# Layer 0 attention as two streams side by side: eight target tiles on ScalarE and GpSimd, seventeen on VectorE

## The chip, the cores and the metric

The kernel runs on one core of a Trainium2 chip. The metric is the device time of one execution in microseconds. TensorE is called PE here (its weight loads PEld), VectorE DVE, ScalarE ACT, GpSimd POOL, and SyncE SP, as in the profile.

## The reference

A graph of 3,125 nodes with 256 features and 103,125 edges passes through four layers. Each layer has a graph attention, a mixing block and an expert network, with layer norms between them. The change is in layer 0, where the graph attention is:

```
proj  = (xn @ Wp.T).reshape(-1, 8, 32)                 # 8 heads
s     = leaky_relu(scores_src[src] + scores_trg[trg], 0.2)
exp_s = exp(s - max(s));  attn = exp_s / (segment_sum(exp_s, trg)[trg] + 1e-16)
out   = segment_sum(proj[src] * attn, trg)
out   = elu(out + xn @ Wskip.T + bias)
x     = x + out + mix(xn)
x     = x + routed_experts(layernorm(layernorm(x)))    # top 2 of 8 experts
```

## The kernel before

The graph is made dense. The function `counts` builds a matrix of how many edges go from each source node to each target node, and stores it in DRAM as bytes, `count_d`, with 25 tiles of 128 source nodes (the last has 53) against all 3,125 targets. Targets are counted in 25 tiles of 125. For some blocks of 250 targets, named by `FAR`, it also stores the counts as bf16 in `far_d`. The order in which blocks are counted is `BLOCKS`.

The attention (`dense_pairs`) then computes, for each pair of heads, the sum over source tiles of (weight matrix) x (projected features `zs`). The weight of an edge is exp of a leaky ReLU of two scores. It can be made in two ways. *Near* (`weigh`, line 1904) uses that exp(leaky_relu(a + b)) is, up to factors that are put elsewhere, the maximum of a row `q` and a column `bar`; one VectorE instruction takes that maximum and multiplies by the counts. *Far* uses logarithms: ScalarE does a Relu (line 1986) and an Exp (line 1987), and GpSimd multiplies by the counts (line 1988).

Before the change there are three chunks of target tiles, `CHUNKS0`: two of 8 and one of 9. In each chunk the first six tiles (750 columns) are near, and the last two or three (250 or 375 columns) far. For each chunk the kernel loops over four pairs of heads; one chunk and one pair of heads is called a unit here, and there are 12. In each unit it loops over 25 source tiles: load the counts, weigh two heads near and two far, and multiply. The matmuls (line 1971) put one head into columns 0 to 63 of the array and the other into 64 to 127, and so go in pairs. The first step of a unit reads the row `q_head` in SBUF; ScalarE then copies it to PSUM (line 1993, `q_near`), and the other 24 steps read it there:

```
q = qs[i][:K] if near is None else near[:K, i, :]
pts.append(self.weigh(wp, q, bar[:K, t, h], a, NQ, K, width=NQ))
```

Only PE's order is written by hand (`manual_schedule`); a scheduler decides that of the other engines. The far products of a step are multiplied one step late. `finish` transposes the sums and divides them (lines 1940 to 1945); its pieces are spread over the next unit's steps. After the four units of a chunk, `then` is called: `gnn0_out` (the skip product, line 739, and an ELU, lines 746 to 852) and `gate0` (two layer norms in one, transposes at line 2600, the router's product with Wr, the two best experts by `first_max`, and their shares, lines 2612 to 2616). It is not written as pieces; the scheduler mixes it with the next chunk's units. After the last chunk comes the routed expert network, which needs every tile's shares; its weights are loaded over the SP and ACT queues when the attention's memory is free.

Of the kernel before, what the change touches and what calls it, by code (L numbers as in the profile page):

```python
# [10 lines left out]
F32 = mybir.dt.float32  # L11
# [38 lines left out]
CHUNKS0 = [(0, 2), (8, 2), (16, 3)]  # L50
FAR = [3, 7, 11, 12]
BLOCKS = [3, 0, 7, 1, 11, 2, 12, 4, 5, 6, 8, 9, 10]
# [1410 lines left out]
class Dense(Net):  # L1463
# [223 lines left out]
    def counts(self, pieces, later):  # L1687
# [4 lines left out]
        self.far_d = self.dram.tile([NS, P, 7 * TP], BF16, name="far_d")  # L1692
# [225 lines left out]
    def dense_pairs(self, att, nodes, then):  # L1918


        nc, tc = self.nc, self.tc
        H, D = 8, 32
        W = D + 1
        NQ = 6 * TP
        zs, bar, q_d, log_s, log_d = nodes
        with ExitStack() as s:
            wq = s.enter_context(tc.tile_pool(name="daq", bufs=4))
            wa = s.enter_context(tc.tile_pool(name="daa", bufs=4))
            wp = s.enter_context(tc.tile_pool(name="dap", bufs=6))
            wo = s.enter_context(tc.tile_pool(name="dao", bufs=3))  # L1930
            we = s.enter_context(tc.tile_pool(name="dae", bufs=2))
            ps_q = s.enter_context(tc.tile_pool(name="dapq", bufs=1, space=PSUM))
            ps_t = s.enter_context(tc.tile_pool(name="dapt", bufs=1, space=PSUM))
            ps = s.enter_context(tc.tile_pool(name="dapp", bufs=4, space=PSUM))

            def finish(os, parts, h0):
                for o, (t, nt) in zip(os, parts):
                    p = ps_t.tile([P, 3, P], F32, name="p_t")[:TP]
                    for k in range(nt):
                        nc.tensor.transpose(p[:, k, :], o[:, k * TP:(k + 1) * TP], self.ident)  # L1940
                    v = p[:, :nt].rearrange("p t (j d) -> p t j d", d=64)
                    inv = wo.tile([TP, 3, 2], F32, name="inv")[:, :nt]
                    nc.vector.tensor_scalar(inv, v[:, :, :, D], 1e-30, None, op0=OP.max)
                    nc.vector.reciprocal(inv, inv)
                    nc.vector.tensor_mul(att[:, t:t + nt, h0 * D:(h0 + 2) * D].rearrange("p t (j d) -> p t j d", d=D),
                                         v[:, :, :, :D], inv[:, :, :, None].to_broadcast([TP, nt, 2, D]))
                    yield

            work = iter(())
            for t0, last in CHUNKS0:  # L1950
                d0, n = t0 * TP, NQ + last * TP
                for h0 in range(0, H, 2):
                    qs, logs = [], []
                    m = n - NQ
                    for i in range(2):
                        qs.append(wq.tile([P, NQ], F32, name="q_head"))
                        nc.sync.dma_start(qs[i], dview(q_d, (h0 + i) * N + d0, [[0, P], [1, NQ]]))
                        logs.append(wq.tile([P, 3 * TP], F32, name="q_log"))
                        nc.sync.dma_start(logs[i][:, :m], dview(log_d, (h0 + i) * N + d0 + NQ, [[0, P], [1, m]]))
                    near = None  # L1960
                    accs = {}

                    def sums(t, K, pts, banks):
                        for b in banks:
                            if t == 0:
                                accs[b] = ps.tile([P, 4, P], F32, name="p_o").rearrange("p a b -> p (a b)")
                            cols = last * TP if b == 2 else 3 * TP
                            for i in range(2):
                                z = (h0 + i) * W
                                at = 0 if b == 2 else b * 3 * TP  # L1970
                                nc.tensor.matmul(accs[b][64 * i:64 * i + 64, :cols], zs[:K, t, z:z + 64], pts[i][:K, at:at + cols],  # L1971
                                                 start=(t == 0), stop=(t == NS - 1))

                    with tc.manual_schedule(engines={mybir.EngineType.PE}):
                        late = None
                        for t in range(NS):
                            a, K = self.count_tile(wa, t, d0, NQ, False, NQ)
                            a_far = wa.tile([P, 3 * TP], BF16, name="a_far")
                            nc.sync.dma_start(a_far[:K, :m], self.far_d[t, :K, t0 // 8 * 250:t0 // 8 * 250 + m])
                            pts, far = [], []  # L1980
                            for i in range(2):
                                h = slice(h0 + i, h0 + i + 1)
                                q = qs[i][:K] if near is None else near[:K, i, :]
                                pts.append(self.weigh(wp, q, bar[:K, t, h], a, NQ, K, width=NQ))
                                f = wp.tile([P, 3 * TP], F32, name="pt_far")
                                nc.scalar.activation(f[:K, :m], logs[i][:K, :m], AF.Relu, bias=log_s[:K, 0, t, h])  # L1986
                                nc.scalar.activation(f[:K, :m], f[:K, :m], AF.Exp, bias=log_s[:K, 1, t, h], scale=1.0 - 0.2)  # L1987
                                nc.gpsimd.tensor_tensor(f[:K, :m], f[:K, :m], a_far[:K, :m], OP.mult)  # L1988
                                far.append(f)
                            if near is None:  # L1990
                                near = ps_q.tile([P, 2, NQ], F32, name="q_near")
                                for i in range(2):
                                    nc.scalar.activation(near[:, i, :], qs[i], AF.Copy)
                            sums(t, K, pts, (0, 1))
                            if late:
                                sums(*late, (2,))
                            late = t, K, far
                            next(work, None)
                        sums(*late, (2,))
                    parts = [(t0, 3), (t0 + 3, 3), (t0 + 6, last)]  # L2000
                    os = []
                    for b, (_, nt) in enumerate(parts):
                        os.append(wo.tile([P, 3 * TP], F32, name="o", bufs=4))
                        nc.scalar.activation(os[b][:, :nt * TP], accs[b][:, :nt * TP], AF.Copy)
                    work = finish(os, parts, h0)
                for _ in work:
                    pass
                then(we, ps, t0, 6 + last)
# [576 lines left out]
    def gate0(self, ps, x, xn, xT, xn_d, gate, t0, nt):  # L2585

        nc = self.nc
        E = 8
        wr, br, g, b, ones, share = gate
        ts = slice(t0, t0 + nt)  # L2590
        with self.tc.tile_pool(name="gate", bufs=1) as w:
            v = w.tile([TP, nt, E], F32, name="score")
            for a, na in GROUPS:
                if t0 <= a < t0 + nt:
                    self.layernorm_twice(xn, x, (a, na))
                    self.part_dma(nc.sync, xn_d.rearrange("(p t) f -> p t f", p=TP)[:, a:a + na, :], xn[:, a:a + na, :])
                    for k in range(KC):
                        p = ps.tile([P, 4, P], F32, name="p_o").rearrange("p a b -> p (a b)")
                        for t in range(na):
                            nc.tensor.transpose(p[:, t * TP:(t + 1) * TP], xn[:, a + t, k * P:(k + 1) * P], self.ident[:TP, :TP])  # L2600
                        nc.vector.tensor_scalar(xT[:, k, a * TP:(a + na) * TP], p[:, :na * TP], g[:, k:k + 1], b[:, k:k + 1],
                                                op0=OP.mult, op1=OP.add)
                    p = ps.tile([P, 4, P], F32, name="p_o").rearrange("p a b -> p (a b)")[:TP, :na * E].rearrange("p (t e) -> p t e", e=E)
                    for t in range(na):
                        self.mm(p[:, t, :], [(xT[:, k, (a + t) * TP:(a + t + 1) * TP], wr[:, k, :]) for k in range(KC)])
                    nc.vector.tensor_add(v[:, a - t0:a - t0 + na, :], p, br[:, None, :].to_broadcast([TP, na, E]))
# [140 lines left out]
    def layers(self, x, xn, xT, out, late):  # L2747
        nc, tc = self.nc, self.tc
        xn_d = self.dram.tile([N, C], F32, name="xn_d")
        with tc.tile_pool(name="hold", bufs=1) as hold:  # L2750
            with tc.tile_pool(name="skip", bufs=1) as sp:
# [8 lines left out]
                def out0(w, ps, t0, nt):  # L2760
                    self.gnn0_out(w, ps, x, xT, xn, skip, t0, nt)
                    self.gate0(ps, x, xn, xT, xn_d, gate, t0, nt)
# [172 lines left out]
```

## Time and profile before

| What | Value |
|---|---|
| Time, median of 3 runs | 5298.61 us (5291.43 to 5307.18) |
| Profiled execution: its own time | 5292.8 us |
| Profiled execution: its span | 5291.0 us |
| Granted PE clock, mean over the span | 0.946 |
| PE, DVE, ACT, POOL busy over the span | 90%, 68%, 31%, 28% |
| Counting of layer 0 | about 125 to 390 us of the span |
| Attention of layer 0, first weigh to last share | 405.8 to 1137.7 us |

A line of the order in time reads: start in us, length in us, engine, line of the kernel, operation, out<-in, shape, and how many instructions were merged into it. Its bracket holds the idle time of the engine before it, and what ended that. In the costliest groups, the mean duration of one instruction contains its waiting inside the engine; how far two starts lie apart is read from the order in time.

### The profile page before, as it was taken

Reading aid. Unit: us, or ns where it says so; the run is one execution under the profiler, and the core shown is the slowest. Engines: PE = TensorE matmul, PEld = TensorE weight load, DVE = VectorE, ACT = ScalarE, POOL = GpSimd, SP = SyncE. Lnnn points to the kernel's source line nnn. Section 1 sums busy time; section 2 is a strip of 40 time slices with the busy share of each in tenths; the row PEclk is TensorE's granted clock in tenths of the full one; section 3 lists DMA queues with packets and bytes.
Section 4 is the critical chain, followed back from the end, with each engine's and each line's share of the span. In section 5 each row is a group of like instructions: output and inputs, shape, how many; then the busy total and the mean of one; then the engine's idle time right before and its main releaser. Section 6 shows DMA issues by size and latency. Waiting matters only on the chain. (4 is left out here: it accounts for less than half of the span.)

```text
span 5291.0 us, 71854 instructions
## 1 busy us (share of the span) xinstructions
PE 4781.0 (90%) x25640; PEld 2885.3 (55%) x25640; DVE 3583.2 (68%) x6095; ACT 1642.1 (31%) x3317; POOL 1507.7 (28%) x1804
## 2 busy tenths in 40 slices
PE   6798999979798899999999899999997888899878
PEld 4565554448654433368645333355665555555557
DVE  6888898865555699845434899932235887777753
ACT  2668787941242100110133000033332111333221
POOL 1206565734300000000001000000004777777733
PEclk8899999979899999999999999999998889999989
DMA  3764333342400111111000111010004656666645
GB/s 92 79 47 115 83 100 83 92 133 65 110 1 0 32 34 43 32 41 35 15 14 1 33 33 42 27 58 8 1 1 120 174 165 185 184 181 171 182 143 173
DMA packets 367496, 413.59 MB, mean 78 GB/s; under 512 B 168554, under 2 KB 300010, under 8 KB 366559
## 3 DMA queue, kind: packets, MB, share of 16 engines
q1 hardware_dynamic: 278794, 189.94, 15.7%
q0 software_dynamic: 53744, 171.34, 11.3%
q10 hardware_dynamic: 34593, 47.63, 2.9%
q8 instruction: 208, 3.41, 0.3%
q14 instruction: 157, 1.28, 0.1%
HBM read 356.74 MB, written 55.18 MB: 78 GB/s over the span
## 5 line engine op out<-in xcount | busy, mean ns | idle before, releaser
L1904 DVE SCALAR_TENSOR_TENSOR pt<-q_head,bar,a 128x750 f32<-128x750 f32 (+2 forms) x824 | 807.4, 1036 | 74.2 <-PE acc L2048 52.3
L2202 POOL DMA_INDIRECT z_edge<-tab,src_i x806 | 776.3, 963 | 266.8 <-issue 210.8
L2043 PE MATMUL acc<-pt,zs 128*64 128x375 f32 (+2 forms) x3200 | 602.6, 501 | 24.2 <-DVE pt L1904 23.9
L2270 PE MATMUL p_acc<-z_edge,oh 128*125 128x264 f32 x2044 | 539.4, 425 | 92.0 <-DVE z_edge L2261 91.7
L1988 POOL TENSOR_TENSOR pt_far<-pt_far,a_far 128x250 f32<-128x250 f32 (+1 forms) x600 | 450.4, 772 | 377.4 <-ACT pt_far L1987 367.5
L1971 PE MATMUL p_o<-pt,zs 128*64 128x375 f32 (+1 forms) x2400 | 527.0, 495 | 30.1 <-DVE pt L1904 29.2
L1904 DVE SCALAR_TENSOR_TENSOR pt<-q_near,bar,a 128x750 f32<-128x750 f32 (+1 forms) x576 | 533.1, 991 | 17.0 <-PE p_o L1971 10.7
L2270 PEld LDWEIGHTS p_acc<-z_edge,oh 128*125 128x125 f32 x2044 | 419.3, 209 | 192.0 <-DVE z_edge L2261 102.2
L2043 PEld LDWEIGHTS acc<-pt,zs 128*64 128x64 f32 (+1 forms) x3200 | 246.4, 136 | 357.1 <-issue 221.0
L1971 PEld LDWEIGHTS p_o<-pt,zs 128*64 128x64 f32 (+1 forms) x2400 | 216.4, 138 | 237.2 <-issue 132.9
L1277 DVE SCALAR_TENSOR_TENSOR x<-p_y,sm,x 125x256 f32<-125x256 f32 x200 | 96.7, 484 | 361.3 <-PE p_y L739 361.3
L1986 ACT ACTIVATE pt_far<-q_log,log_s 128x250 f32<-128x250 f32 (+1 forms) x600 | 290.0, 529 | 89.7 <-PE p_o L1971 74.3
L1971 PE MATMUL p_o<-pt_far,zs 128*64 128x250 f32 (+3 forms) x1200 | 313.2, 414 | 2.1 <-POOL pt_far L1988 2.0
L2048 PE MATMUL acc<-pt,zs 128*32 128x375 f32 (+2 forms) x3200 | 313.4, 497 | 0.0
L1987 ACT ACTIVATE pt_far<-pt_far,log_s 128x250 f32<-128x250 f32 (+1 forms) x600 | 287.6, 524 | 0.2
L2098 PE MATMUL acc<-zs,pt 128*125 128x257 f32 x1250 | 275.6, 383 | 11.7 <-issue 11.7
L2098 PEld LDWEIGHTS acc<-zs,pt 128*125 128x125 f32 x1250 | 234.7, 189 | 52.6 <-issue 14.5
L1261 ACT ACTIVATE h<-p_tr,bn 128x500 f32<-128x500 f32 (+1 forms) x224 | 161.8, 723 | 296.7 <-PE p_tr L739 296.7
L2261 DVE TENSOR_TENSOR z_edge<-z_edge,near_e 128x2112 f32<-128x2112 f32 (+1 forms) x101 | 236.5, 2341 | 18.6 <-ACT near_e L2253 18.6
L2057 ACT ACTIVATE o<-acc 128x375 f32<-128x375 f32 (+1 forms) x48 | 21.2, 493 | 608.3 <-DMA q_head<-q_g 330.3
L1063 POOL IOTA own<- 5x256 f32 x1 | 0.4, 356 | 720.7 <-PE acc L2048 720.7
L1904 DVE SCALAR_TENSOR_TENSOR pt<-q_all,bar,a 128x500 f32<-128x500 f32 (+3 forms) x175 | 119.1, 683 | 122.6 <-PE acc L2098 120.2
(547 smaller groups left out, 7856.6 us busy)
## 6 DMA issues: line engine op xcount, KB each, us to landing
a<-count_d SPq DMA_DIRECT2D x432, 93.8 KB
row<-dst_row SPq DMA_DIRECT2D x101, 224.0 KB
ef<-in_edge_s SPq DMA_DIRECT2D x101, 128.0 KB
z_edge<-tab,src_i POOLq DMA_INDIRECT x806
a_far<-far_d SPq DMA_DIRECT2D x192, 62.5 KB
count_d<-stage SPq DMA_DIRECT2D x12, 781.2 KB
q_head<-q_g SPq DMA_DIRECT2D x24, 375.0 KB
a_far<-far_d SPq DMA_DIRECT2D x96, 93.8 KB
```

The costliest lines, as they stand in the source:

```text
L1261: nc.scalar.activation(o[:, m, :n], p[:, :n], AF.Relu, bias=b[:, e, m:m + 1], scale=g[:, e, m:m + 1])
L1904: self.nc.vector.scalar_tensor_tensor(pt[:K, :n], q, bar, a[:K, :n], op0=OP.max, op1=OP.mult)
L1971: nc.tensor.matmul(accs[b][64 * i:64 * i + 64, :cols], zs[:K, t, z:z + 64], pts[i][:K, at:at + cols], start=(t == 0), stop=(t == NS - 1))
L1986: nc.scalar.activation(f[:K, :m], logs[i][:K, :m], AF.Relu, bias=log_s[:K, 0, t, h])
L1987: nc.scalar.activation(f[:K, :m], f[:K, :m], AF.Exp, bias=log_s[:K, 1, t, h], scale=1.0 - 0.2)
L1988: nc.gpsimd.tensor_tensor(f[:K, :m], f[:K, :m], a_far[:K, :m], OP.mult)
L2043: nc.tensor.matmul(acc[i // 2][64 * (i % 2):64 * (i % 2) + 64, b, :b1 - b0], zs[:K, t, i * W:i * W + 64], pts[i][:K, b0:b1], **st)
L2048: nc.tensor.matmul(acc[2][32 * i:32 * i + 32, b, :b1 - b0], zs[:K, t, z:z + 32], pts[i][:K, b0:b1], **st)
L2098: nc.tensor.matmul(acc[i], pt[:K, i * TP:(i + 1) * TP], zs[:K, t, :C + 1], start=(t == 0), stop=(t == NS - 1))
L2202: nc.gpsimd.indirect_dma_start(out=zs[i][:, j, :], out_offset=None, in_=table, in_offset=bass.IndirectOffsetOnAxis(ap=src[:, c0 + j:c0 + j ...
L2261: nc.vector.tensor_mul(zh, zh, weight[:, :, :, None].to_broadcast([P, n, H, D + 1]))
L2270: nc.tensor.matmul(acc[t], ohs[i, t][:, k - a, :], zs[i][:, k - c0, :HW], start=(k == cols[t][0]), stop=(k == cols[t][1] - 1))
```

## The change

The weighing becomes two streams. The near stream has the tiles 16 to 24 and then 8 to 15 (`NEAR0`), all on VectorE, with weighs of 1,125 and 1,000 columns: 8 units of 25 steps. The far stream has the tiles 0 to 7 (`FAR0`), with ScalarE instructions and GpSimd products of 1,000 columns: 4 units of 25 steps. One loop over the 200 near steps issues a far step whenever 9n >= 16m, so that the 100 far steps are spread over the first 178 near ones. The order on all five engines is now written by hand. Products are multiplied one step late in both streams. The copy of `q` to PSUM is gone: PSUM holds three banks of near sums, two of far sums, one for the transposes and two for the outputs. The outputs (`outputs0` in place of `gnn0_out` and `gate0`) are a generator, and each near step runs one piece of it or of `finish`. `FAR` and `BLOCKS` are set so that the blocks needed first are counted first. The diff, cut to its core:

```diff
-CHUNKS0 = [(0, 2), (8, 2), (16, 3)]
-FAR = [3, 7, 11, 12]
-BLOCKS = [3, 0, 7, 1, 11, 2, 12, 4, 5, 6, 8, 9, 10]
+NEAR0 = ((16, 9), (8, 8))
+FAR0 = (0, 8)
+FAR = [0, 1, 2, 3]
+BLOCKS = [0, 8, 1, 9, 2, 10, 3, 11, 12, 4, 5, 6, 7]
...
+            wq = s.enter_context(tc.tile_pool(name="daq", bufs=3))
             wa = s.enter_context(tc.tile_pool(name="daa", bufs=4))
+            wp = s.enter_context(tc.tile_pool(name="dap", bufs=4))
...
+            def finish(accs, t0, nt, h0):
+                os = []
+                for acc, (a, k) in zip(accs, split(nt)):
+                    os.append(wo.tile([P, 4 * TP], F32, name="o", bufs=4))
+                    nc.scalar.activation(os[-1][:, :k * TP], acc[:, :k * TP], AF.Copy)
...
+                turns.append(rest())
+                if h0 + 2 == H:
+                    ends.append(then(we, ps, t0, nt))
...
+            def near_weigh(n):
+                u, t = divmod(n, NS)
+                (_, nt), h0 = near[u]
+                a, K = counts.pop(n)
+                pts[n] = [self.weigh(wp, qs[u, i][:K], bar[:K, t, h0 + i:h0 + i + 1], a, nt * TP, K, width=9 * TP) for i in range(2)]
...
+            def far_weigh(m):
...
+                for i in range(2):
+                    h = slice(2 * u + i, 2 * u + i + 1)
+                    f = wp.tile([P, nq], F32, name="pt_far")
+                    nc.scalar.activation(f[:K], logs[u, i][:K], AF.Relu, bias=log_s[:K, 0, t, h])
+                    nc.scalar.activation(f[:K], f[:K], AF.Exp, bias=log_s[:K, 1, t, h], scale=1.0 - 0.2)
+                    nc.gpsimd.tensor_tensor(f[:K], f[:K], a[:K], OP.mult)
+                    out.append(f)
...
+                for n in range(NN + 1):
+                    if n < NN:
+                        u, t = divmod(n, NS)
+                        near_weigh(n)
+                        if n + 3 < NN:
+                            near_counts(n + 3)
+                        if t in (12, NS - 1) and u + 1 < len(near):
+                            near_rows(u + 1, int(t > 12))
+                    if m <= NF and 9 * n >= 16 * m:
+                        if m < NF:
+                            far_weigh(m)
+                            if m + 2 < NF:
+                                far_counts(m + 2)
...
+                        if m:
+                            far_sums(m - 1)
+                        m += 1
+                    if n:
+                        near_sums(n - 1)
+                    piece()
+                while turns or ends:
+                    piece()
...
+    def outputs0(self, w, ps, x, xn, xT, xn_d, skip, gate, t0, nt):
...
+        for k in range(nt + 4):
+            if k >= 4:
+                t = t0 + k - 4
+                nc.vector.scalar_tensor_tensor(xn[:, t, :], es.pop(k - 4), 1.0, xn[:, t, :], op0=OP.min, op1=OP.add)
+                nc.vector.scalar_tensor_tensor(x[:, t, :], xn[:, t, :], -1.0, x[:, t, :], op0=OP.add, op1=OP.add)
+                st = self.norms.tile([TP, nc.vector.BN_STATS_DIM], F32, name="bn_st")
+                nc.vector.bn_stats(st, x[:, t, :])
+                nc.vector.bn_aggr(mv[:, k - 4, :], st)
...
+            yield
+        rstd = w.tile([TP, 9], F32, name="rstd")
+        nc.scalar.activation(rstd[:, :nt], mv[:, :nt, 1], AF.Sqrt, bias=self.eps10[:TP], scale=1.0 + 1e-5)
...
+        for t in range(nt):
+            self.mm(p[:, t, :], [(xT[:, k, (t0 + t) * TP:(t0 + t + 1) * TP], wr[:, k, :]) for k in range(KC)])
...
+            m, one = self.first_max(w, v, "12"[i])
+            tops.append(m)
+            nc.vector.tensor_copy(ones[:, i, ts, :], one)
...
-                self.dense_pairs(xn, nodes, out0)
+                self.dense_pairs(xn, nodes, lambda w, ps, t0, nt: self.outputs0(w, ps, x, xn, xT, xn_d, skip, gate, t0, nt))
```

## The prediction

> **What bounds the kernel now.** I read the stretches of the attention first, then its costliest groups, then the order in time around single instructions, and last the stretch that hands over to the routed layer. The stretches' columns are: length, busy time of PE, PEld, DVE, ACT and POOL (with counts), granted PE clock, DMA share, GB/s.
>
> ```profile
> 405.00:1100.00 695.00, 656.54 (x3887) 341.16 (x3887) 619.95 (x845) 585.92 (x1300) 451.07 (x604) 0.96 0.36 93
> 1100.00:1138.00 38.00, 27.73 (x116) 19.68 (x113) 25.88 (x92) 13.11 (x27) 0.74 (x3) 0.76 0.49 165
> 1138.00:1167.00 29.00, 11.55 (x52) 7.32 (x52) 17.93 (x51) 0.00 (x0) 4.63 (x9) 0.50 0.69 226
> ```
>
> The weighing runs from 405 to 1100 with four engines nearly full; the last outputs end at 1138, and then routing starts. In steady state VectorE sets the step:
>
> ```profile
> 701.56 10.96 DVE L1904 SCALAR_TENSOR_TENSOR pt<-q_near,bar,a 128x750 f32<-128x750 f32 x12
> 704.12 1.28 POOL L1988 TENSOR_TENSOR pt_far<-pt_far,a_far 128x250 f32<-128x250 f32 x2 [0.40 <-PE p_o L1971]
> 705.80 1.28 POOL L1988 TENSOR_TENSOR pt_far<-pt_far,a_far 128x250 f32<-128x250 f32 x2 [0.40 <-ACT pt_far L1987]
> ```
>
> Twelve weighs in 10.96 us are 0.91 each, two per step of some 1.82; GpSimd's two products take 0.64 each beside them, and neither slows the other. That holds because q stands in PSUM (q_near). The first weighs of a unit still read q_head in SBUF, and there the picture is another:
>
> ```profile
> 405.78 1.91 DVE L1904 SCALAR_TENSOR_TENSOR pt<-q_head,bar,a 128x750 f32<-128x750 f32 x2 [12.32 <-DMA a_far<-far_d]
> 452.51 0.98 DVE L1904 SCALAR_TENSOR_TENSOR pt<-q_head,bar,a 128x750 f32<-128x750 f32 x1
> 452.60 1.41 POOL L1988 TENSOR_TENSOR pt_far<-pt_far,a_far 53x250 f32<-53x250 f32 x1
> 453.42 2.02 DVE L1904 SCALAR_TENSOR_TENSOR pt<-q_head,bar,a 128x750 f32<-128x750 f32 x1
> 453.98 0.66 POOL L1988 TENSOR_TENSOR pt_far<-pt_far,a_far 128x250 f32<-128x250 f32 x1
> ```
>
> At 405.78 no product runs: the pair takes 1.91. At 452.51 the first weigh takes 0.98 and the product beside it 1.41 instead of 0.65; then two products run, and the second weigh takes 2.02. The two engines take turns. The pair ends at 455.44, 2.93 after its start, where the four parts alone sum to 0.91 + 0.64 + 0.64 + 0.98 = 3.17: nearly a full sum, less 0.08 at each of three hand-overs. Ten of the eleven pairs after 405.78 take 2.3 to 3.3 us.
>
> **What the change costs.** Every near weigh now reads q_head from SBUF; the PSUM copy (L1993, 24 copies of 0.79 on ACT) is gone, and its banks hold the second stream's sums. So all near weighs and all far products must take turns. Their sizes by these rows:
>
> ```profile
> 1091.81 1.75 POOL L1988 TENSOR_TENSOR pt_far<-pt_far,a_far 128x375 f32<-128x375 f32 x2 [0.23 <-PE p_o L1971]
> 3332.04 4.24 DVE L1904 SCALAR_TENSOR_TENSOR pt<-q_head,bar,a 128x875 f32<-128x875 f32 x4
> 1901.06 2.11 PE L2043 MATMUL acc<-pt,zs 128*64 128x375 f32 x12
> ```
>
> *VectorE.* 875 wide, q in SBUF: (4.24 - 1.12) / 3 = 1.04; 750 wide 0.92; so about 0.125 per 125 columns. 1,000 wide 1.17, 1,125 wide 1.30. 200 of each (4 head pairs x 25 source tiles x 2 heads): 494 us, against 600 x 0.91 = 546 before. *GpSimd.* 250 wide 0.64, 375 wide 0.875, so 0.235 per 125: 1,000 wide 2.05. It is 200 products now instead of 600: 410 us. *Taking turns:* 904. The outputs inside the stream bring two instructions per tile with two SBUF inputs (as L852 and L749, 0.34 apart when free), 17 tiles: 11. Hand-overs give back: both queues run until their buffers are empty (two steps of pt, two of pt_far), so some 100 hand-overs by 0.08: -8.
>
> The rest of VectorE's work in the stream reads PSUM or one SBUF input: 26 splits of finish by 0.7 (L1943 to L1945), 17 tiles by 1.1, and 7 for xT and first_max, 43 in all. GpSimd can use that time when it has work; I take 10 of 0 to 43. At each of seven unit changes near_rows of the second head waits on SP for the last weigh of the old row (three buffers), and the next counts stand behind it; before, the first row took 10.8 us from issue (392.95) to its reader (403.77). GpSimd has up to two far steps (8 us) to run meanwhile: I take 5 of 0 to 60. Stream: 904 + 11 - 8 + 10 + 5 = **922**. Before, first weigh to end of the last: 405.8 to 1097.0, 691. **+231.**
>
> *What lies beside it.* TensorE: 12 matmuls of 375 take 2.11, so a pair on two column groups comes every (2.11 - 0.48) / 5 = 0.33; a 9-tile step needs 1.96, an 8-tile or far step 1.74: 200 near and 100 far steps 544, with some 56 for transposes, skip products and gate, 600 of 922. Hidden, at a price if its clock falls (rival 3). In its hand-written queue far_sums stands ahead of near_sums, so near buffers can wait for GpSimd; that is a wait inside the turns, as GpSimd holds them just then. ScalarE: pairs of 250 take 0.90, of 375 1.10, so 1,000 wide is some 0.95 apart; 400 of them 380 us, hidden; finish's copies queue behind at most four of these, and TensorE waits for them at unit changes inside its slack. Loads: 144 KB per near and 256 KB per far step, 512 KB in some 9.2 us or 56 GB/s, under the 93 shown. The gate's casts move from GpSimd to VectorE (two of 0.2 per chunk) and its Sqrt table loads (1.28) into ScalarE's slack: nothing. Counts: far copies grow from 7 tiles to 8, some 4 us on ACT, busy 174 of 265 there: 0 to 4, I take 0. First weigh: the counts of the first chunk are written earlier by the new BLOCKS; 0 to 5 gained, I take 2.
>
> *The tail* grows: the far outputs begin only after step 178 and do not end before the last near sums, so their gate stands ahead of the eight near tiles' outputs, where before nine tiles were left:
>
> ```profile
> 1095.05 1.90 DVE L1904 SCALAR_TENSOR_TENSOR pt<-q_near,bar,a 53x750 f32<-53x750 f32 x2 [2.63 <-DMA a<-count_d]
> 1131.12 2.84 PE L739 MATMUL p_o<-w_L_ffn_Wr,xT 128*125 128x8 f32 x12 [0.56 <-DVE xT L2601]
> 1137.49 0.17 DVE L2616 TENSOR_TENSOR share<-mx,share 125x9 f32<-125x9 f32 x1
> ```
>
> Before: 1097.0 to 1137.7, 40.7. After, in VectorE's built order: last sums, copies and near finish 6; far's xn, transposes and xT 8; its 32 Wr matmuls by 0.237, 7.5; two first_max and the exp 5; then eight near tiles by 1.7 (skip matmuls 1.8 apart per tile on PE) with filling 18; ACT's weight loads stand between their exps (before, four w2 issues lasted 9.3), +6; rstd with its table load 2; the same xn, Wr and maxima again 18. Sum 70, **+29**; 45 if PE, ACT and DVE overlap better, 95 if the loads hold ACT. From share on, routing follows as before.
>
> Sum: 231 + 29 - 2 = +258 on the profiled execution, 5292.8 (span 5291.0): 5551; on the median of 5298.6, 5.8 higher, it would be 5557. I say **5550**.
>
> **Rules against rows.** The row at 453.98 shows a product that began while a weigh had waited since 453.42. The Trainium skill, "SBUF — State Buffer", section "Who interferes with whom", says that a VectorE instruction with two SBUF inputs and a GpSimd one that reads SBUF exclude each other for the whole instruction, and whoever issues first wins. By strict issue order there would be about 400 hand-overs instead of 100, and the sum 24 lower; the row speaks for bursts.
>
> The row 1138 to 1167 shows a clock of 0.50 with PE busy 11.55 of 29. "TensorE: Matmul & The Clock Gate", section "What's actually happening", has the clock halve after an idle window of about 3.4 us. By it GpSimd's bursts of 4 us could halve it half of the time, and PE's work in the stream would be some 900 instead of 600.
>
> **Rivals.** *1, no turns at this width:* the engines overlap as at 704. For it: 704 to 712, but that is with q in PSUM. Then PE bounds: 100 x (1.96 + 9/16 x 1.74) + 78 x (1.74 + 0.98) + 22 x 2.34 (VectorE alone) = 294 + 212 + 51 = 557, +56 = 613; 691 falls by 78, +29 - 2: -51, **5242**. Against it: every product beside a weigh from q_head. It decides if fewer than some 115 of GpSimd's 410 us have to wait (494 + 11 + 43 + 115 = 663, at which 663 - 691 + 27 is nothing). *2, half the turns:* half of each product fits beside the weighs. For it: three pairs of 2.3 to 2.4 with products near; against it: at 503.05 the four products beside a pair of 2.40 took 4.41 instead of 2.6, and at 921.90 three beside a pair of 1.89 took 4.19 instead of 2.65, so there it was they that waited. 494 + 205 + 25 = 724, +33 + 27: **5353**. *3, the bursts cost TensorE too:* its waits lower the clock. For it: 0.50 in the row 1138 to 1167, 0.76 in the tail; against it: 0.96 in the weighing. At 0.7 its 600 are 860, and with each far step's 1.74 and the 60 at unit changes no longer hidden, 922 + 60 + 60 = 1042: **5670**. *Change without its effect:* not possible here, since the built order has 400 weighs from q_head and 200 products of 1,000.
>
> **Chances.** Forecast (5480 to 5620) 0.79, rival 1 0.06, rival 2 0.05, rival 3 0.10. Range 5450 to 5650: POOL's extrapolated width (5% is 20 us), the 0 to 60 at unit changes, the tail's 45 to 95, and half of rival 3; it leaves out rivals 1 and 2, the rest of 3 and 0.04 of the forecast. A measurement tells 0.3% (16 us) from none. Faster 0.06, same 0.01, slower 0.93.
>
> **What would show it.** Right: weighs of 1,125 with means of 1.6 to 2.6 us instead of 1.38, products of 2.5 to 4 instead of 2.1, PE busy some 65% of the stream, last weigh near 1320, share near 1390. Wrong: weighs of 1.4 beside products of 2.1 and PE over 95% (rival 1); PE clock under 0.8 in the stream (rival 3); a first weigh after 415 or a tail over 95 us (my small terms).

## The result, and the profile after

The changed kernel takes 5550.91 us (median of 4 runs, 5547.14 to 5563.43), the kernel before beside it 5302.03 (5291.43 to 5307.18): ratio 1.0476, 95% interval 1.0452 to 1.0501. The profiled execution has a span of 5551.3 us.

The stretches of the attention in the changed kernel, columns as before (length; busy time of PE, PEld, DVE, ACT, POOL; granted PE clock; DMA share; GB/s):

```profile
390.00:500.00 110.00, 83.38 (x360) 36.61 (x360) 104.78 (x45) 61.67 (x57) 80.21 (x27) 0.86 0.28 85
500.00:1249.00 749.00, 592.07 (x2438) 224.99 (x2438) 725.87 (x464) 398.89 (x391) 503.89 (x174) 0.92 0.25 72
1249.00:1324.00 75.00, 70.43 (x245) 23.67 (x244) 64.92 (x91) 9.42 (x20) 0.55 (x1) 0.94 0.11 29
1324.00:1392.00 68.00, 51.95 (x159) 34.80 (x158) 35.37 (x114) 12.41 (x24) 0.19 (x1) 0.51 0.61 200
```

The weighing now runs from 390.4 to 1324.1, 933.7 us instead of 691. VectorE is busy 97% of the long stretch, GpSimd 67%, TensorE 79%. The busy time of VectorE and GpSimd is not work alone: an instruction's length contains its waiting for the other engine. The groups of the stream (busy time, then the mean of one in ns):

```profile
L2033 POOL TENSOR_TENSOR pt_far<-pt_far,a_far 128x1000 f32<-128x1000 f32 x192 | 555.9, 2919 | 407.2 <-ACT pt_far L2032 181.3 <-DMA a_far<-far_d 143.1 <-PE p_n L1957 80.4
L1905 DVE SCALAR_TENSOR_TENSOR pt<-q_head,bar,a 128x1125 f32<-128x1125 f32 x192 | 447.2, 2397 | 25.5 <-DMA a<-count_d 16.8 <-PE p_n L1957 7.1 <-DMA q_head<-q_g 1.5
L1905 DVE SCALAR_TENSOR_TENSOR pt<-q_head,bar,a 128x1000 f32<-128x1000 f32 x192 | 349.4, 1876 | 21.7 <-PE p_n L1957 20.7 <-DMA q_head<-q_g 1.0
```

Means hide the pattern here. The weighs (tile pt) and the products (tile pt_far) between 690 and 707 us show it; the three figures are the shortest, the median and the longest in ns:

```profile
L1905 DVE SCALAR_TENSOR_TENSOR pt<-q_head,bar,a x6: 3199/3210/3221, 688.9 to 704.5; 128x1125 f32<-128x1125 f32 x6
```
```profile
L2033 POOL TENSOR_TENSOR pt_far<-pt_far,a_far x6: 2481/3162/3240, 687.6 to 703.4; 128x1000 f32<-128x1000 f32 x6
```

One weigh, one product, one weigh, one product: all six weighs and four of the six products last about 3.2 us, because each contains the other engine's instruction (the other two products, 2.48, had come later, after a wait for ScalarE). A product alone is 2.07 (the shortest of the stream) and a weigh alone 1.39. No weigh of the whole stream lasts over 3.24, so VectorE never waits for more than one product at a time. GpSimd does, in two of its 200 products:

```profile
L2033 POOL TENSOR_TENSOR pt_far<-pt_far,a_far x200: 2069/3042/8256, 397.8 to 1247.5; 128x1000 f32<-128x1000 f32 x96, 53x1000 f32<-53x1000 f32 x4
1239.66 5.92 DVE L1905 SCALAR_TENSOR_TENSOR pt<-q_head,bar,a 128x1000 f32<-128x1000 f32 x5
1256.76 4.77 DVE L1905 SCALAR_TENSOR_TENSOR pt<-q_head,bar,a 128x1000 f32<-128x1000 f32 x4 [10.41 <-PE p_n L1957]
```

The longest product, 8.26, starts at 1239.26 and ends at 1247.52; the five weighs from 1239.66 on, begun after it, go ahead of it. TensorE's order has the far sums before the near ones, so VectorE then waits 10.41 us for TensorE, its longest wait inside the stream.

### The profile page after: what moved, and what is told of

It reads as the page before. It is cut to its first block, busy times and chain, and to the rows that moved or that the text cites. A ratio compares the mean times of both kernels' runs of the same rounds, so it can differ in the third digit from the quotient of the medians.

```text
span 5551.3 us, 67765 instructions
## 1 busy us (share of the span) xinstructions
PE 4906.9 (88%) x24840; PEld 2852.3 (51%) x24840; DVE 3870.0 (70%) x5869; ACT 1525.5 (27%) x2485; POOL 1639.5 (30%) x1398
## 4 chain that ended last, share of the span: by engine, by line
PE 56%; DVE 20%; issue 10%; POOL 7%; DMA 5%; ACT 2%; DVEq 0%; ACTq 0%; POOLq 0%; SPq 0%; another core or an unknown queue 0%
DVE pt L1905 11%; PE acc L2120 10%; PE p_tr L740 7%; PE acc L2125 5%; PE acc L2175 5%; PE p_acc L2347 4%; PE p_y L740 4%; PE p_a L740 3%; POOL z_edge L2279 3%; PE p_h L740 2%; PE p_q L740 2%; PE p_n L1957 2%; DMA z_edge<-tab,src_i 2%; PE p_kvt L740 1%; PE p_t L740 1%
## 5 line engine op out<-in xcount | busy, mean ns | idle before, releaser
L1905 DVE SCALAR_TENSOR_TENSOR pt<-q_head,bar,a 128x750 f32<-128x750 f32 (+5 forms) x1200 | 1600.5, 1392 | 108.1 <-PE acc L2125 52.3
L1957 PE MATMUL p_n<-pt,zs 128*64 128x375 f32 (+3 forms) x2000 | 560.5, 580 | 181.3 <-DVE pt L1905 179.3
L2033 POOL TENSOR_TENSOR pt_far<-pt_far,a_far 128x1000 f32<-128x1000 f32 (+1 forms) x200 | 584.6, 2948 | 410.2 <-ACT pt_far L2032 184.2
L1957 PEld LDWEIGHTS p_n<-pt,zs 128*64 128x64 f32 (+1 forms) x2000 | 181.8, 147 | 497.2 <-DVE pt L1905 293.7
L2031 ACT ACTIVATE pt_far<-q_log,log_s 128x1000 f32<-128x1000 f32 (+1 forms) x200 | 223.7, 1119 | 307.5 <-PE p_f L1957 278.0
L1957 PE MATMUL p_f<-pt_far,zs 128*64 128x500 f32 (+1 forms) x800 | 259.3, 628 | 16.2 <-POOL pt_far L2033 16.1
L2032 ACT ACTIVATE pt_far<-pt_far,log_s 128x1000 f32<-128x1000 f32 (+1 forms) x200 | 225.7, 1129 | 6.5
L2125 PEld LDWEIGHTS acc<-pt,zs 128*32 128x32 f32 (+1 forms) x3200 | 85.0, 109 | 202.8 <-issue 201.5
```

What stands on the lines that cost most here:

```text
L1905: self.nc.vector.scalar_tensor_tensor(pt[:K, :n], q, bar, a[:K, :n], op0=OP.max, op1=OP.mult)
L1957: nc.tensor.matmul(accs[b][64 * i:64 * i + 64, :k * TP], zs[:K, t, z:z + 64], pts[i][:K, a * TP:(a + k) * TP], start=(t == 0), stop=(t == ...
L2031: nc.scalar.activation(f[:K], logs[u, i][:K], AF.Relu, bias=log_s[:K, 0, t, h])
L2032: nc.scalar.activation(f[:K], f[:K], AF.Exp, bias=log_s[:K, 1, t, h], scale=1.0 - 0.2)
L2033: nc.gpsimd.tensor_tensor(f[:K], f[:K], a[:K], OP.mult)
L2125: nc.tensor.matmul(acc[2][32 * i:32 * i + 32, b, :b1 - b0], zs[:K, t, z:z + 32], pts[i][:K, b0:b1], **st)
```

## The experiments

The runs were made in several sets. In those of runs 1 to 9 the kernel before itself takes 5575 to 5593 us, so each ratio is against the kernel before in the same set, and times inside the attention are set against each other. The totals named in the expectations of runs 1 to 4 count from 5298.6; as ratios they are 1.051 to 1.057, 0.987, 0.987 to 0.993, and 1.009. The theory is that VectorE with two SBUF inputs and GpSimd take turns.

**1. The kernel before, with q in SBUF.**

```
-  q = qs[i][:K] if near is None else near[:K, i, :]
-  pts.append(self.weigh(wp, q, ...))
+  pts.append(self.weigh(wp, qs[i][:K], ...))
   ... (the copy to q_near left out)
```

> The kernel before, with one edit: every weigh reads q_head in SBUF, and the copy to PSUM is left out. Theory (VectorE with two SBUF inputs and GpSimd take turns): 600 weighs x 0.92 + 400 products x 0.64 + 200 x 0.875 = 552 + 431 = 983 us instead of a stream of 691, less up to 300 hand-overs x 0.08 = 24: about 5570 to 5600 us, weighs with means over 1.3 us. Rival (the two hand-written streams of the changed kernel, their queues and sizes, cost the time, and where q stands does not matter): 5290 to 5310, since none of that is in this kernel.

Measured: 5812.24, ratio 1.0429 (1.0395 to 1.0463). The stream takes 931 us instead of 691. Its groups:

```profile
L1904 DVE SCALAR_TENSOR_TENSOR pt<-q_head,bar,a 128x750 f32<-128x750 f32 x576 | 776.4, 1410 | 31.1 <-PE p_o L1969 16.9 <-DMA a_far<-far_d 12.6 <-DMA a<-count_d 1.0
L1985 POOL TENSOR_TENSOR pt_far<-pt_far,a_far 128x250 f32<-128x250 f32 x384 | 494.9, 1324 | 200.7 <-DMA a<-count_d 135.7 <-ACT pt_far L1984 64.6
```

A weigh of 750 columns rises from 0.99 to 1.41 on the mean, a product of 250 columns, 0.65 alone, to 1.32. None of the new queues, sizes or streams is in this kernel, and yet nearly the whole loss is. The loss of 237 us is 35 to 65 under what was expected. Each hand-over gives a little back, and I had taken at most 300 of them; in the trace 528 of the 600 weighs and 544 of the 600 products last longer than alone, some 770 hand-overs more, which at 0.08 are 62 us.

**2. The changed kernel without the product.**

```
-  nc.gpsimd.tensor_tensor(f[:K], f[:K], a[:K], OP.mult)
```

> The changed kernel without GpSimd's product: the far weights go to TensorE without their counts, all loads are kept (the output is another one). Theory (turns): weighs fall to 1.3 to 1.4 (1,125 wide) and 1.17 to 1.25 (1,000 wide), the stream from 934 to about 613, which TensorE sets, and the total from 5551 to about 5230. Rival (hand-written queues: far_sums ahead of near_sums, loads behind waits on SP): ScalarE's chain and the queues stay, so the stream stays over 800 and the total over 5420.

Measured: 5522.80, ratio 0.9904 (0.9867 to 0.9940). The stream takes 622 us (expected 613), with the same queues, loads and activations:

```profile
450.00:980.00 530.00, 527.73 (x2641) 245.24 (x2637) 475.96 (x511) 408.41 (x408) 0.00 (x0) 1.00 0.35 106
```

TensorE is busy 527.7 of 530 us: it sets the pace once the turns are gone. The rival of the hand-written queues (a stream over 800) falls.

**3. The changed kernel with all products, and q in PSUM.** What reads q is the only thing that differs in the turns: GpSimd does what it did.

```
+  q_bank = ps_q.tile([P, 4, TP], F32, name="q_bank")
...
-  pts[n] = [self.weigh(wp, qs[u, i][:K], ...) for i in range(2)]
+  if t == 0: ... nc.scalar.activation(q_bank[:, 2 * (u % 2) + i, :], qs[u, i][:, :TP], AF.Copy)
+  nc.vector.scalar_tensor_tensor(pt..., q_bank[:K, 2 * (u % 2) + i, None, :].to_broadcast([K, nt, TP]), ...)
```

> The changed kernel, all products kept, but the near weighs read q from PSUM: 125 columns per head are copied there once a unit and read again for every tile (so the near weights are computed with the first tile's q), and the outputs have one PSUM bank instead of two. Theory (turns come from VectorE's second SBUF input): products back to about 2.1 us and weighs to 1.3 or less, stream 613 to 640, total 5230 to 5260. Rival (the 1,000-wide products or ScalarE's chain are simply too slow, or the queues hold each other): 5540 or more, since GpSimd does the same work in the same order.

Measured: 5578.20, ratio 1.0005 (0.9988 to 1.0022); the stream takes 676 us.

```profile
L2045 POOL TENSOR_TENSOR pt_far<-pt_far,a_far 128x1000 f32<-128x1000 f32 x192 | 402.6, 2097 | 318.1 <-DMA a_far<-far_d 144.5 <-ACT pt_far L2044 138.1 <-issue 9.8
L2007 DVE SCALAR_TENSOR_TENSOR pt<-q_bank,bar,a 128x1125 f32<-128x1125 f32 x192 | 254.8, 1384 | 56.8 <-PE p_n L1959 35.6 <-ACT q_bank L2003 19.1 <-DMA a<-count_d 2.1
```

Products fall from 2.92 to 2.10 and weighs from 2.40 to 1.38, side by side, with the counts still read from SBUF by both engines. So it is VectorE's second SBUF input that makes the turns, and neither the width nor ScalarE's chain. The stream misses 613 to 640: VectorE waits 35.6 for TensorE and 19.1 for the unit's copies in the 1,125-wide half alone, and with one output bank the tail is 78 (67 with two, in run 2). Stream and tail make 754 against 691 + 41 = 732 before; an earlier start (first weigh 387.6) makes up for most of it, and the totals are level.

**4. Half of the products** (for the first head of each pair only).

```
+  if i == 0:
       nc.gpsimd.tensor_tensor(f[:K], f[:K], a[:K], OP.mult)
```

> The changed kernel with GpSimd's product for the first head of each pair only (the other head's far weights lack their counts). Theory (turns, full sum): 100 products x 2.05 = 205 us less: 934 - 205 = 729 for the stream, total about 5345. If only part of each product waits or is waited for (engines overlap in part until TensorE's 613 binds), the step from the whole to the half would be larger than from the half to none; if the queues or ScalarE hold the stream, under 5 us are gained: over 5540.

Measured: 5645.12, ratio 1.0137 (1.0106 to 1.0167); the stream takes 748 us (expected 729).

```profile
L2034 POOL TENSOR_TENSOR pt_far<-pt_far,a_far 128x1000 f32<-128x1000 f32 x96 | 261.8, 2727 | 520.5 <-ACT pt_far L2032 286.9 <-DMA a_far<-far_d 143.4 <-PE p_n L1957 81.1
```

From none to half of the products the stream grows by 748 - 622 = 126 us, from half to whole by 934 - 748 = 186. That is the pattern which the expectation gave to an overlap in part, until TensorE binds. It does not take a second mechanism: with no products TensorE binds, and VectorE is busy 559 of 622. From these 559 a hundred products of 2.16, less the 0.17 that each hand-over gives back (both below; in the trace 97 weighs and 79 products waited), make 745, near the 748. The second hundred cost 1.86 each, most of a product's 2.1.

**5. Two streams with q_near.** An attempt at a faster version.

```
-NEAR0 = ((16, 9), (8, 8))
+NEAR0 = ((19, 6), (13, 6), (8, 5))
...
+  q = ps_q.tile([P, 2, 6 * TP], F32, name="q_near")   # copied at t == 0 of a unit; two banks for near sums, one for outputs
...
+  near_sums(n - 1), then far_weigh(m), far_counts, far_sums(m - 1)
```

> The two streams with q back in PSUM: near chunks of 6, 6 and 5 tiles (300 steps of two weighs), q_near in three banks as before (the first step of a unit reads SBUF), two banks each for the near and the far sums, one bank for outputs and transposes, near_sums and its copies ahead of far_weigh. Theory (turns): 400 weighs x 0.92 + 200 x 0.8 = 530 us on VectorE with some 70 beside them, TensorE some 610, no turns but in 12 first steps (about +1 each): a stream of 620 to 660 and, with five tiles left for the tail, 45 to 60 there: share 25 to 60 us earlier than before, ratio 0.988 to 0.996. Rival (two hand-written streams as such cost the time): a ratio over 1.02.

Measured: 5587.72, ratio 1.0008 (0.9988 to 1.0029). Products are at 2.13 and weighs at 0.99. Of the turns some 14 us are left: the first weighs of a unit (1.25 on the mean), and six of 50 additions of the outputs with two SBUF inputs, which last 1.1 to 2.2 instead of 0.42. Two hand-written streams as such do not cost the 243 us. The tail is 47 as expected. The stream, though, takes 710 and not 620 to 660:

```profile
500.00:600.00 100.00, 98.90 (x536) 45.74 (x533) 90.64 (x112) 81.73 (x80) 73.21 (x35) 1.00 0.40 106
600.00:700.00 100.00, 89.65 (x438) 37.30 (x436) 90.50 (x129) 64.07 (x72) 52.33 (x24) 0.98 0.30 81
```

Without outputs TensorE is full; with them (600 to 700) it stands for 10 of 100 us. Over the whole stream it is busy 668 of 710 us, where I had counted some 610, and that is most of the miss. What makes it stand was not tested: between 600 and 700 it waits 6.0 us for weighs and 0.9 for additions that empty the one bank of the skip products.

**6. The outputs in pieces alone**, in the kernel before.

```
-  ps = ... bufs=4
+  ps = ... bufs=3;  ps_o = ... bufs=1
...
+  if next(work, self) is self:
+      next(ends, None)
...
-  then(we, ps, t0, 6 + last)
+  ends = then(we, ps_o, t0, 6 + last)      # outputs0, run inside the next chunk
```

> The kernel before, its weighs, products and chunks kept; of the change only the outputs in pieces: outputs0 of a chunk runs piece by piece inside the next chunk, with a PSUM bank of its own (the sums have three instead of four). Theory (turns cost everything, pieces are harmless): the two chunk changes in the stream lose their outputs (some 20 to 40 us in all), sums with three banks wait a little for their copies at 11 unit changes (0.5 to 2 us each), the tail grows by the skip products done in steps (0 to 25 us): ratio 0.993 to 1.002. Rival (the outputs in pieces are what costs): over 1.02.

Measured: 5600.43, ratio 1.0026 (1.0005 to 1.0048), a little over the expected range.

```profile
410.40:1094.00 683.60, 655.30 (x3871) 324.02 (x3871) 619.98 (x845) 584.51 (x1291) 450.66 (x596) 0.98 0.37 94
1094.00:1154.00 60.00, 42.23 (x132) 24.89 (x129) 28.83 (x89) 14.40 (x31) 3.75 (x6) 0.59 0.06 20
```

The stream gains 8 us (684 against 691, not 20 to 40) and the tail loses 19 (60 against 41): nine tiles in a fixed order of steps through one bank take longer there than the old outputs did. The pieces explain part of the changed kernel's longer tail, and none of its 243 us in the stream.

**7. The earlier start.** The changed kernel weighs first at 390.4, the kernel before at 405.8; I had allowed 0 to 5. Before (first two rows GpSimd, the last TensorE):

```profile
218.25 8.49 POOL L1872 COPY log_s<-es 128x200 f32<-128x200 f32 x1 [50.19 <-DVE es L1868]
227.52 0.84 POOL L1626 DMA_DIRECT2D gate<-in_L_mix_Wqkv  x1
240.92 5.19 PE L739 MATMUL p_a<-gate,xT 128*125 128x512 f32 x6 [12.89 <-DMA gate<-in_L_mix_Wqkv]
```

After:

```profile
217.16 0.80 POOL L1627 DMA_DIRECT2D gate<-in_L_mix_Wqkv  x1 [48.97 <-ACT zs L1868]
219.30 4.30 POOL L1873 COPY log_s<-es 128x200 f32<-128x200 f32 x1 [1.34 <-DVE es L1869]
```

A load of 512 KB stood behind two GpSimd instructions; now it is issued ahead of them, 10.4 us earlier, and TensorE's 12.89 for it are gone. The 8.49 us of the first of them look like turns too: from 218.11 to 226.53 VectorE runs six one-hot instructions with two SBUF inputs, 1.46 to 1.48 each and none of them delayed, and the copy ends 0.2 us after the last. In the trace of run 7 the same copy takes 1.56. To test the load, the kernel before with that load on SyncE:

```
-  self.nc.gpsimd.dma_start(wkv, ...)
+  (self.nc.sync if name == "gate" else self.nc.gpsimd).dma_start(wkv, ...)
```

> The kernel before; the load of the key weights for the folding (tile gate, in keys_weight) is issued by SyncE instead of GpSimd, where it stands behind the two log_s instructions. Theory (the changed kernel starts weighing 15 us earlier because there this load is issued ahead of the log_s instructions, and the wait of 12.9 us for it is gone): first weigh near 393 instead of 406, and the total 10 to 15 us lower (ratio 0.997 to 0.998). Rival (the new order of the counted blocks and the earlier far blocks make the earlier start): first weigh at 404 to 408, ratio 1.000.

Measured: first weigh at 398.4, where the two kernels with the old beginning (runs 1 and 6) have 408.6 and 410.4: 10 to 12 us earlier, though not the 393 expected, and the wait for this load is gone. The total, 5581.13 and ratio 0.9991 (0.9972 to 1.0010), does not tell so little. With the beginning of the changed kernel (runs 2 to 4) the first weigh is at 387.6 to 388.4, so the load is about half of that kernel's earlier start. The rest stays open; in runs 8 to 11 small edits of the order put it anywhere from 388.6 to 404.1.

**8. A version meant to be faster:** pieces for the first two chunks, the old outputs for the last, the load on SyncE.

```
+  if t0 < 16: ... ends = then(we, ps_o, t0, 6 + last)
+  else: ... last_then(we, ps, t0, 6 + last)          # gnn0_out and gate0 of the kernel before
```

> A version meant to beat both kernels: the kernel before with (1) the outputs of its first two chunks in pieces inside the next chunk, as in the run with the pieces alone, (2) the outputs of the last chunk at once as before, so that its tail of 41 us is kept instead of 60, and (3) the key weights' load issued by SyncE. Theory: first weigh 10 us earlier, stream 684 instead of 691, tail about 41: share 17 us earlier, ratio 0.996 to 0.998. Rival (what the pieces save in the stream is given back in the tail, whatever its form): tail over 50 us, ratio 0.998 to 1.002.

Measured: first weigh 388.6, earlier than expected; stream 683 and tail 43, about as expected. The total, 5587.65 and ratio 0.9988 (0.9964 to 1.0012), cannot be told from none; its interval only just reaches the 0.996 to 0.998 named.

**9. The bias added by VectorE.** The kernel before has, ahead of the weighing, the plainest case of the turns. GpSimd, then VectorE:

```profile
152.22 15.84 POOL L1785 TENSOR_TENSOR x<-x,r_L_mix_bproj 125x6400 f32<-125x6400 f32 x1 [42.96 <-DMA r_L_mix_bproj<-in_L_mix_bproj]
```
```profile
154.62 14.76 DVE L1736 TENSOR_TENSOR oh_key<-key_t,is_key 128x2520 bf16<-128x2520 bf16 x1
```

Over all oh_key instructions the median is 1.46.

```
-  nc.gpsimd.tensor_add(x, x, bproj[:, None, :].to_broadcast([TP, NT, C]))
+  nc.vector.tensor_add(x, x, bproj[:, None, :].to_broadcast([TP, NT, C]))
```

> The version with pieces for the first two chunks, whole outputs for the last and the load on SyncE, and one more edit: the addition of the projection's bias to x (125x6400 f32, before the weighing, 14 to 16 us on GpSimd) is done by VectorE. In the kernel before, one oh_key instruction of VectorE (two SBUF inputs) stands 14.76 us beside it instead of 1.46. Theory (a VectorE instruction with two SBUF inputs waits for the whole GpSimd instruction): no oh_key or oh_lo over 2 us is left, VectorE pays some 7 us for the addition (by 0.98 us for 128x800 f32), and counting ends some 6 us earlier: first weigh at 380 to 385, total ratio 0.994 to 0.997. Rival (the long oh_key is a wait for something else, such as the one-hot's buffers): an instruction of some 14 us stays, first weigh at 388 or later, ratio 0.997 to 1.000.

Measured: 5582.20, ratio 0.9989 (0.9965 to 1.0013). The stall is gone (longest oh_key 1.47, longest oh_lo 1.49; the addition takes 6.82), but the first weigh comes at 404.1, later than in run 8 and than the 380 to 385 expected. VectorE's timeline where the stall was:

```profile
154.21 1.46 DVE L1736 TENSOR_TENSOR oh_key<-key_t,is_key 128x2520 bf16<-128x2520 bf16 x1
165.16 1.49 DVE L1733 TENSOR_TENSOR oh_lo<-lo_t,is_lo 128x2560 bf16<-128x2560 bf16 x1 [9.48 <-PE p_cnt L1749]
```

It ran ahead into the next wait: TensorE waits for ScalarE's far copies, and these 10.6 us for the one far buffer to be written out.

**10 and 11. The far blocks counted every third instead of every second**, once on top of run 8 and once on top of run 9.

```
-BLOCKS = [3, 0, 7, 1, 11, 2, 12, 4, 5, 6, 8, 9, 10]
+BLOCKS = [3, 0, 1, 7, 2, 4, 11, 5, 6, 12, 8, 9, 10]
```

> As the version with pieces for the first two chunks and the load on SyncE, with one more edit: the blocks whose counts also go to the far stream are counted every third (BLOCKS = 3, 0, 1, 7, 2, 4, 11, 5, 6, 12, 8, 9, 10) instead of every second, since ScalarE waits 14.7 us for the one far buffer to be written out. If those waits are on the path: first weigh 3 to 8 us earlier than 388.6, ratio 0.996 to 0.998. If not: 387 to 390, ratio 0.998 to 1.000.

> The same spacing together with the bias added by VectorE. In the run with the bias on VectorE the 14.8 us stall was gone, but VectorE waited 9.48 for TensorE, that for ScalarE, and that 10.6 for the far buffer's way out. Theory (the stall was only replaced by that wait): with the spacing the first weigh comes at 380 to 386, ratio 0.994 to 0.997. Rival (the start is set by something else): 395 or later, ratio 0.998 or more.

Measured, in a set where the kernel before takes 5300.03: 5289.95, ratio 0.9979 (0.9968 to 0.9990), and 5281.42, ratio 0.9959 (0.9944 to 0.9974). Both beat both kernels, the kernel before by 0.2% and 0.4%. The waits for the far buffer are gone in both, but the load on SyncE now came late, and this line is new against run 7 (in the second of them):

```profile
PE p_a L739 <- DMA gate<-in_L_mix_Wqkv: 16.8, 1, 16.8
```

So the first weighs come at 402.6 and 393.6, later than any time I had named for run 10 and than the 380 to 386 for run 11. Between the two the bias on VectorE is worth 9 us, once the far buffer does not take them back. Streams (680 and 683) and tails (43 in both) are as in run 8.

## Why the prediction was right, and where its steps were off

The total (5550 against 5550.91) rests on the step that decided it: near weighs from q_head and far products take turns. Runs 1, 2 and 3 show it from three sides. That it agrees to 1 us is luck: against the forecast the stream is 12 us longer, the tail 2 shorter, the start 13 earlier, and what follows share 6 longer; and within the stream two larger misses cancel. By its terms:

- **VectorE and GpSimd, 904.** The weighs were right: by the reading of the prediction four weighs alone of 1,125 (5.29, run 2) and of 1,000 (4.77, run 2 and the row above) give (5.29 - 1.39) / 3 = 1.30 and (4.77 - 1.25) / 3 = 1.17, as predicted. The product was mis-sized: run 3 has four alone in 8.63, 2.16 each, where 2.05 was extrapolated from 250 and 375 columns. The sum is 200 x 1.30 + 200 x 1.17 + 200 x 2.16 = 926, 22 more than predicted.
- **Hand-overs, -8.** This step was wrong in kind. I read bursts from one row of the kernel before; the changed kernel mostly alternates one for one. In the row pair above six weighs start from 688.9 to 704.5, one every 15.6 / 5 = 3.12 us, where a weigh and a product alone take 1.30 + 2.16 = 3.46: a hand-over saves 0.17, not 0.08. In the whole stream 187 weighs and 182 products last longer than alone, so there were some 370 hand-overs: about -63. The mis-sized product and the miscounted hand-overs partly cancelled: 926 - 63 = 863 against 904 - 8 = 896.
- **The rest of the stream, 26** (11 + 10 + 5). To reach 933.7 it must be about 71. VectorE's own account says where it is. It is busy 896 us of the stream (the stretches above), 825 of them in weighs: 494 for weighing, as predicted, and 331 waiting for GpSimd, where 410 - 8 = 402 were predicted. Its other work takes 70, and for 38 it is idle (27.8 of these for TensorE, 10.41 of them in the one wait above, 3.7 for counts, 2.5 for rows of q). So GpSimd cost 71 us less than predicted, as part of it ran beside this other work and idle time, and the rest 82 more. These shares are read from the trace, not tested.
- **Tail, 70 predicted, 67.5 measured** (1324.1 to 1391.6). The cause was only partly the one given. ScalarE's loads, priced at 6, do not hold it: while the near tiles' skip products run, ScalarE waits for VectorE. TensorE's clock adds to it instead (0.51 in the last stretch above). Each of the eight skip products takes TensorE 3.14 us, back to back, instead of the 1.8 I took:

```profile
1343.49 2.05 PE L740 MATMUL p_o<-w_L_gnn_Wskip,xT 128*125 128x256 f32 x4
1345.47 1.21 PE L740 MATMUL p_o<-r_L_gnn_bias,ones 1*125 1x256 f32 x2
1346.61 2.07 PE L740 MATMUL p_o<-w_L_gnn_Wskip,xT 128*125 128x256 f32 x4
```

In the tail of the kernel before the same two groups take 1.13 and 0.69, and the granted clock from 1101 to 1115.6 is 1.00:

```profile
1105.53 1.13 PE L739 MATMUL p_o<-w_L_gnn_Wskip,xT 128*125 128x256 f32 x4
1106.59 0.69 PE L739 MATMUL p_o<-r_L_gnn_bias,ones 1*125 1x256 f32 x2
```

So the eight products take some 25 us instead of the 14 predicted for them: misses of the tail's sum cancel too.

- **Start, -2 predicted, -15.4 measured.** I looked at which counts are written first, not at GpSimd's queue, where a load had moved ahead of two instructions (run 7). Of the three parts of the sum this misses by most, and it is outside its 0 to 5.
- **After share, 0 predicted, some 6 measured.** Share ends 253.9 later, but the edge attention starts 260 later. In the unchanged TensorE-bound stage before it the granted clock is 0.97 to 0.98 in the first 200 us, where the kernel before has 1.00; why, no run shows.

The rivals: *no turns* (1) and *half the turns* (2), streams of 613 and 724, are excluded by the 933.7 and by the weighs' and products' lengths. *The clock* (3) is there in small: TensorE's clock is 0.92 in the long stretch instead of 0.96, a 375-wide matmul takes 0.54 on the mean (0.48 in run 2), and TensorE is busy 80% of the stream instead of the 65% foretold. It costs little: TensorE still waits 294 us for weighs, and VectorE's waits for TensorE, 27.8 us, are all that the trace shows of a cost.

**Rules against rows, again.** Here a rule was set aside for one row, wrongly. The Trainium skill, "SBUF — State Buffer", section "Who interferes with whom", has whoever issues first win the port and keep it for the whole instruction. With each engine's next instruction already queued, that gives the one-for-one alternation of 690 to 707, and the 14.76 us shown with run 9 are its largest single case. The rule's 400 hand-overs at the measured 0.17 would have made the term -68, near the -63 worked out above. But the row at 453.98 was no accident either: of the ten delayed pairs at the starts of units in the kernel before, four have a second weigh of 2.0 us that waited for two products, as there, and six one of 1.4 to 1.65 that waited for one. GpSimd too is passed by more than one instruction, at 1239.26 (five weighs) and at 218.25 (VectorE's one-hot instructions). So the trace had both patterns before the change. What decides between them stays open.

## What to carry to other kernels

Before widening work on GpSimd, list which of VectorE's instructions beside it read two SBUF operands: in these runs their times added, at widths from 250 to 1,125 columns and with both ways of queueing. One operand in PSUM removed it, so a PSUM copy that looks like overhead (q_near, 24 copies of 0.79) was worth 237 us in run 1. And when a stall is removed, look for the wait just behind it (the far buffer in run 9, the load in runs 10 and 11): it can give back what was won.

## What the runs showed of the hardware that I had not expected

- VectorE (two SBUF inputs) and GpSimd mostly alternate one instruction for one when both have work queued, and a hand-over costs nothing: the two overlap by some 0.17 us. It is not a fixed order: a GpSimd product stood 8.26 us while five weighs begun after it went ahead.
- A VectorE instruction with two bf16 SBUF inputs, 1.46 us alone, stood 14.76 beside one GpSimd addition of 15.84 us: the wait is for the whole instruction.
- VectorE with one input in PSUM and one in SBUF ran beside GpSimd's 1,000-wide products with no loss that the means show: 1.384 against 1.387 with no products at all.
